# Router logits from a second, transposed copy of the input, and a first stage in a written order

## The chip, the cores and the metric

The kernel runs on one core of a Trainium2 chip, as one program. The metric is the device time in microseconds of that core: 2810.78 us, the median of three runs (2807.64 to 2812.17).

## The reference, cut to what matters

The input `x` has 32 batches of 128 x 1024 values in fp32. Two layers follow each other, each added to its own input.

```python
def _L0_cond_ref(x, conditions, weights):
    w = weights[conditions]                      # one 128 x 128 matrix per batch
    return jnp.einsum('bct,bcd->bdt', x, w)      # h = w^T x, per batch

def _moe(hidden_states, gate_w, wg, wu, wd):     # E = 64 experts, K = 8, CAP = 256
    logits = x @ gate_w.T                        # x here is h, 4096 tokens x 1024
    probs = jax.nn.softmax(logits, axis=-1)
    w, sel = jax.lax.top_k(probs, K)
    w = w / jnp.sum(w, axis=-1, keepdims=True)
    ...                                          # each expert takes its first 256 tokens
    h = silu(inp @ wg) * (inp @ wu)
    out = h @ wd                                 # scattered back, weighted by w

x = x + moe(cond(x))
x = x + L1_ffn(L1_cond(x))                       # dense 1024 x 1024 maps with low-rank terms
```

In the second layer two linear maps follow each other, `L1_cond_W` and the maps of `L1_ffn` (the kernel calls these side by side `head_w`). The kernel multiplies the two sets of weights with each other once, and applies the product to the tokens. These products of weights are called the combined weights here; they have nothing to do with the tokens.

## The kernel before, in words

A token is a row of `h`; a batch gives 128 tokens. The work has three stages.

**First stage** (lines 228 to 352). It runs over 8 groups of 4 batches. For a batch, GpSimd fetches the 128 x 128 matrix `w_b` by an indirect DMA, and the SP queue loads `x_t` (512 KB). The input is copied to `ybuf` in device memory, which collects the layer's sum. TensorE computes `h = w_b^T x` in two halves of 512 columns (`ph`, line 271), ScalarE copies both halves out (line 272), and the result is stored to `hbuf`, from which the experts gather their tokens. For the router logits the hidden size must lie on the partitions, so TensorE turns each of the 8 column blocks of `h` (`pt`, line 280), VectorE copies them out as `hT` (line 281), and 8 matmuls per batch with `hT` as the stationary operand give `plog` (line 283). Once per group come the top 8 of 64 logits, the weights `wt`, the ranks of the tokens within each expert (`prk`, lines 322 and 325), their store to `ranks`, and the counts (`pcnt`, line 333), which are added up in `upto`.

The combined weights are made in blocks of columns. Blocks 0 and 1 belong to this stage (lines 344 to 352): 9 products of 8 matmuls each per block (`pcw`, line 210). They are written last in the source, in order; a scheduler puts single matmuls of them between the batches' work. Their results gather in one tile, `CWa`, which a DMA stores to `cwbuf` once per block (line 352). A third block is made much later.

Order: of this stage nothing is kept in the order of the source. The scheduler may move an instruction on its engine wherever its operands allow. Instructions wrapped by `kept` or by the class `InOrder` (lines 213 to 225) stay in the order in which the source issues them; before, of these early parts only the VectorE object `dve` and the indirect DMAs of the lookup are wrapped, from the second stage on.

**Between the stages** (lines 575 to 603) the kernel finds which tokens the first experts take: `looked_up` (VectorE, from `upto`), `fetched` (8 indirect DMAs from `ranks`), `found` (VectorE, and one small matmul `prow`, line 438, that brings the row numbers to the right partitions), `placed`, `gathered` (8 indirect DMAs from `hbuf` per expert), and `columns` (VectorE turns the gathered tokens into `xT`). `token_sums` and `weight_sums` form the sums of half blocks with which the 8 products of a 2 x 2 block multiplication become 7 (`s`, `t` tiles).

**Second stage**: a loop over 64 experts, TensorE products `pp` (line 519) and `po` (line 630), with a prefetch of the next expert's three weights of 1.5 MB into tiles of two buffers per tag, `wg`, `wu` and `wd`. The operands of the combined weights use the same tags, so an expert's weight loads wait until these are read. **Third stage**: 16 pairs of batches through the second layer; neither changes.

Of the kernel before, what the change touches and what calls it, by code (L numbers as in the profile page):

```python
# [9 lines left out]
I32 = mybir.dt.int32  # L10
# [41 lines left out]
def kernel(  # L52
# [6 lines left out]
    gate_wT: bass.AP,  # L59
# [65 lines left out]
    for q in range(1, NQ):  # L125
# [22 lines left out]

    adapter_i = const.tile([P, NB], I32, name="adapter_i")
    nc.sync.dma_start(adapter_i, adapter.to_broadcast([P, NB]))  # L150
    scal_bc = const.tile([P, E2], F32, name="scal_bc")
    nc.sync.dma_start(scal_bc, scal.to_broadcast([P, E2]))
    adapter_rows = const.tile([P, NB], I32, name="adapter_rows")
    nc.vector.tensor_scalar(adapter_rows, adapter_i, float(P), pcol, ALU.mult, ALU.add)
    adapter_f = const.tile([P, NB], F32, name="adapter_f")
    nc.vector.tensor_copy(adapter_f, adapter_i)
    smask = const.tile([P, NB, E2], F32, name="smask")
    nc.vector.tensor_tensor(
        smask,
        adapter_f.unsqueeze(2).to_broadcast([P, NB, E2]),  # L160
        iota_t[:, 0:E2].unsqueeze(1).to_broadcast([P, NB, E2]),
        ALU.is_equal,
    )
    nc.vector.tensor_tensor(
        smask, smask, scal_bc.unsqueeze(1).to_broadcast([P, NB, E2]), ALU.mult
    )

    own = const.tile([P, HC], F32, name="own")
    nc.vector.tensor_scalar(own, iota_t[:, 0:HC], float(Q), inquad, ALU.mult, ALU.add)
    far = const.tile([P, 1], F32, name="far")  # L170
    nc.vector.tensor_scalar(far, quad, float(W4), None, ALU.mult)
    nc.vector.tensor_scalar(own, own, far, None, ALU.add)

    rb_bc = const.tile([P, E2], F32, name="rb_bc")
    nc.sync.dma_start(rb_bc, router_b.to_broadcast([P, E2]))
# [30 lines left out]
    def multiplied(n, d, hw, left, pool, tag, pe):  # L206
        w = BLOCKS[n][1] - BLOCKS[n][0]
        pcw = pool.tile([P, 512], F32, name=f"pcw_{n}_{d}", tag=tag)[:, 0:w]
        for j in range(HC):
            pe.matmul(pcw, left[d][:, j, :], hw[:, j, :], start=(j == 0), stop=(j == HC - 1))  # L210
        return pcw
# [13 lines left out]
    dve = InOrder(nc.vector)  # L225


    with (
        tc.tile_pool(name="a1", bufs=1) as a1,
        tc.tile_pool(name="a3", bufs=3) as a3,  # L230
        tc.tile_pool(name="a2", bufs=2) as a2,
        tc.tile_pool(name="pa_big", bufs=3, space=PSUM) as pa_big,
        tc.tile_pool(name="pa_sm", bufs=2, space=PSUM) as pa_sm,
        tc.tile_pool(name="pa_cw", bufs=2, space=PSUM) as pa_cw,
    ):
        gw_sb = a1.tile([P, HC, E], F32, name="gw_sb")
        nc.sync.dma_start(gw_sb, gate_wT.rearrange("(j p) e -> p j e", p=P))

        zeros = a1.tile([P, 256], F32, name="zeros")
        nc.vector.memset(zeros, 0.0)  # L240
        for buf in (hbuf, ybuf):
            nc.scalar.dma_start(
                buf[NT : NT + P, :].rearrange("p (n c) -> p n c", c=256),
                zeros.unsqueeze(1).to_broadcast([P, H // 256, 256]),
            )
        pad = a1.tile([E, 2, P], F32, name="pad")
        nc.vector.memset(pad[:, 0, :], float(NT))
        nc.vector.memset(pad[:, 1, :], 0.0)
        nc.scalar.dma_start(ranks[:, NB, :, :], pad)

        for g in range(NB // GB):
            plog = pa_sm.tile([P, GB, E], F32, name=f"plog_{g}", tag="sm")
            for t in range(GB):
                b = g * GB + t
                rows = slice(b * P, (b + 1) * P)
                w_b = a3.tile([P, P], F32, name=f"w_{b}", tag="w_b")
                nc.gpsimd.indirect_dma_start(
                    out=w_b,
                    out_offset=None,
                    in_=cond_w,  # L260
                    in_offset=bass.IndirectOffsetOnAxis(ap=cond_rows[:, b : b + 1], axis=0),
                )
                x_t = a3.tile([P, H], F32, name=f"x_{b}", tag="x_t")
                nc.sync.dma_start(x_t, x[b])
                nc.scalar.dma_start(ybuf[rows, :], x_t)

                h_sb = a2.tile([P, H], F32, name=f"h_{b}", tag="h_sb")
                for n in range(2):
                    cols = slice(n * 512, (n + 1) * 512)
                    ph = pa_big.tile([P, 512], F32, name=f"ph_{b}_{n}", tag="big")  # L270
                    nc.tensor.matmul(ph, w_b, x_t[:, cols], start=True, stop=True)  # L271
                    nc.scalar.copy(h_sb[:, cols], ph)
                nc.scalar.dma_start(hbuf[rows, :], h_sb)

                hT = a2.tile([P, HC, P], F32, name=f"hT_{b}", tag="hT")
                for n in range(2):
                    pt = pa_big.tile([P, 4, P], F32, name=f"pt_{b}_{n}", tag="big")
                    for j in range(4):
                        c = n * 4 + j
                        nc.tensor.transpose(pt[:, j, :], h_sb[:, c * P : (c + 1) * P], ident)  # L280
                    nc.vector.tensor_copy(hT[:, n * 4 : n * 4 + 4, :], pt)
                for j in range(HC):
                    nc.tensor.matmul(  # L283
                        plog[:, t, :],
                        hT[:, j, :],
                        gw_sb[:, j, :],
                        start=(j == 0),
                        stop=(j == HC - 1),
                    )
# [744 lines left out]
```

## Time and profile before

| What | Value |
|---|---|
| Median of 3 runs | 2810.78 us |
| The profiled execution: its own time, its span | 2809.41 us, 2807.7 us |
| Mean granted TensorE clock | 0.993 |
| Busy share of the span: TensorE, VectorE, ScalarE, GpSimd | 98%, 57%, 15%, 40% |
| HBM read, written | 442.90 MB, 123.83 MB |
| `ph` matmuls up to 310 us (records, busy) | 128, 69.0 us |
| `plog` matmuls up to 310 us | 512, 61.2 us |
| `pt` transposes up to 310 us | 256, 38.9 us |
| `pcw` matmuls up to 310 us | 288, 102.9 us |
| `hT` copies on VectorE, `h` copies on ScalarE | 64 x 688 ns, 64 x 587 ns |

The span runs from the first to the last instruction of the profiled execution; its own time is 1.7 us longer than the span. A line of a view names the source line, the engine, the tile written and the tile read. An fp32 matmul stands as two records, a transpose as one. A record's busy time [...] overlaps the next record, so how long a row of matmuls takes is read from the distance between their starts, or from the chain of waits, and not from busy times.

### The profile page before, as it was taken

To read this page: it belongs to the slowest core of one execution; us is meant where nothing else is said; L and a number is where in the kernel's file an instruction comes from. 1 tells how busy PE (TensorE), PEld (TensorE's weight loads), DVE (VectorE), ACT (ScalarE), POOL (GpSimd) and SP (SyncE) were. 2 spreads that over 40 slices of the span, in tenths; PEclk is the share of its full clock that TensorE was granted. 3 is DMA by queue.
4 is the path that set the end of the run, shared out by engine and by line. 5 is a ranking of instruction groups with operands and counts; after the bars stand their busy time and mean duration, and the time that the engine had idled before them with its cause. 6 is when DMAs were issued, how large, how long until landed. Compare 5 with 4: busy or idle time off the path is not lost.

```text
span 2807.7 us, 23998 instructions
## 1 busy us (share of the span) xinstructions
PE 2744.9 (98%) x8772; PEld 1516.8 (54%) x8772; DVE 1598.3 (57%) x2545; ACT 427.2 (15%) x824; POOL 1112.2 (40%) x846
## 2 busy tenths in 40 slices
PE   6998999999999999999999999999999899999999
PEld 4774555555555555555555555555555545555554
DVE  2443566676666766667666666666664344444443
ACT  1220111111111111112111111111111000000000
POOL 1114164655646555464554655556451100000000
PEclk9999999999999999999999999999999999999999
DMA  9873577877878787787877877778775532222210
GB/s 354 309 268 131 177 250 228 252 252 236 255 226 253 243 243 259 224 254 234 247 259 232 253 227 245 255 236 258 221 241 160 135 75 64 64 64 64 64 46 38
DMA packets 130789, 568.33 MB, mean 202 GB/s; under 512 B 23600, under 2 KB 50288, under 8 KB 105328
## 3 DMA queue, kind: packets, MB, share of 16 engines
q1 hardware_dynamic: 67040, 373.72, 36.7%
q0 software_dynamic: 51200, 155.24, 23.7%
q10 hardware_dynamic: 12432, 37.85, 3.5%
q8 instruction: 69, 1.13, 0.2%
q14 instruction: 48, 0.39, 0.0%
HBM read 442.90 MB, written 123.83 MB: 202 GB/s over the span
## 4 chain that ended last, share of the span: by engine, by line
PE 95%; DMA 3%; issue 1%; DVE 1%; POOL 0%; ACT 0%; SPq 0%; ACTq 0%; DVEq 0%
PE pp L519 41%; PE po L630 23%; PE pr_c L223 17%; PE pcw L210 3%; PE px L223 2%; PE pcw L223 2%; PE plog L283 2%; PE ph L271 2%; PE pth L569 1%; PE pt L280 1%; DMA hbuf<-h 1%; DMA hw<-in_head_w 1%; PE prk L325 0%; PE prk L322 0%; DMA xq<-ybuf 0%
## 5 line engine op out<-in xcount | busy, mean ns | idle before, releaser
L456 POOL DMA_INDIRECT xin<-hbuf,slot_row x512 | 715.1, 1397 | 209.1 <-issue 152.7
L630 PE MATMUL po<-wd,hTb 128*128 128x512 f32 x1536 | 680.3, 592 | 0.6 <-ACT hTb L571 0.6
L641 POOL DMA_INDIRECT ybuf<-o,slot_tok x128 | 204.3, 1596 | 665.2 <-ACT o L639 468.0
L630 PEld LDWEIGHTS po<-wd,hTb 128*128 128x128 f32 x1536 | 286.8, 190 | 323.7 <-issue 306.1
L519 PE MATMUL pp<-wg,xT 128*128 128x384 f32 x1024 | 351.3, 486 | 0.0
L519 PE MATMUL pp<-t,s 128*128 128x384 f32 x1024 | 344.6, 490 | 5.2 <-DVE t L223 5.2
L519 PEld LDWEIGHTS pp<-t,s 128*128 128x128 f32 x1024 | 194.6, 191 | 148.8 <-issue 31.2
L519 PEld LDWEIGHTS pp<-wg,xT 128*128 128x128 f32 x1024 | 189.6, 190 | 119.0
L223 DVE TENSOR_TENSOR u<-p,pp 128x384 f32<-128x384 f32 x64 | 35.4, 553 | 381.4 <-PE pp L519 381.4
L639 ACT ACTIVATE o<-po,slot_w 128x512 f32<-128x512 f32 x256 | 175.9, 687 | 494.5 <-PE po L630 494.5
L223 POOL DMA_INDIRECT ab<-in_AT,adapter_rows x32 | 36.5, 1142 | 449.4 <-ACT pxw L223 444.0
L223 PE MATMUL pr_c<-BM,X 128*128 128x512 f32 x480 | 213.7, 592 | 0.0
L223 DVE STREAM_TRANSPOSE xT<-xin 128x1024 f32<-128x1024 f32 x128 | 155.9, 1233 | 75.5 <-DMA xin<-hbuf,slot_row 65.0
L519 PE MATMUL pp<-t,xT 128*128 128x384 f32 x512 | 175.6, 486 | 0.0
L519 PE MATMUL pp<-wu,xT 128*128 128x384 f32 x512 | 175.6, 486 | 0.0
L519 PE MATMUL pp<-wu,s 128*128 128x384 f32 x512 | 175.6, 486 | 0.0
L536 ACT ACTIVATE h<-gate 128x384 f32<-128x384 f32 x128 | 67.0, 523 | 704.7 <-DVE gate L223 704.7
L392 POOL DMA_INDIRECT rkg<-ranks,row x128 | 123.1, 962 | 71.9 <-issue 38.4
L223 PE MATMUL pr_c<-ts,ss 128*128 128x512 f32 x320 | 142.5, 592 | 1.3 <-DVE ss L223 1.3
L223 PEld LDWEIGHTS pr_c<-BM,X 128*128 128x128 f32 x480 | 88.9, 190 | 100.2 <-issue 100.0
L223 DVE TENSOR_TENSOR u<-u,pp 128x384 f32<-128x384 f32 x128 | 70.4, 550 | 126.9 <-PE pp L519 126.9
L519 PEld LDWEIGHTS pp<-t,xT 128*128 128x128 f32 x512 | 97.3, 190 | 67.8
(159 smaller groups left out, 2990.4 us busy)
## 6 DMA issues: line engine op xcount, KB each, us to landing
wd<-in_wd SPq DMA_DIRECT2D x64, 1536.0 KB, 7.3
wg<-in_wg SPq DMA_DIRECT2D x64, 1536.0 KB, 6.9
wu<-in_wu SPq DMA_DIRECT2D x64, 1536.0 KB, 9.4
x<-in_x SPq DMA_DIRECT2D x32, 512.0 KB, 5.1
ybuf<-x ACTq DMA_DIRECT2D x32, 512.0 KB, 4.9
hbuf<-h ACTq DMA_DIRECT2D x32, 512.0 KB, 5.5
xq<-ybuf SPq DMA_DIRECT2D x64, 256.0 KB, 5.1
out_y<-out_c SPq DMA_DIRECT2D x32, 512.0 KB, 2.7
```

Of the source, the lines that this page charges most:

```text
L210: pe.matmul(pcw, left[d][:, j, :], hw[:, j, :], start=(j == 0), stop=(j == HC - 1))
L223: return lambda *args, **kw: kept(op(*args, **kw))
L271: nc.tensor.matmul(ph, w_b, x_t[:, cols], start=True, stop=True)
L280: nc.tensor.transpose(pt[:, j, :], h_sb[:, c * P : (c + 1) * P], ident)
L283: nc.tensor.matmul(plog[:, t, :], hT[:, j, :], gw_sb[:, j, :], start=(j == 0), stop=(j == HC - 1),)
L392: nc.gpsimd.indirect_dma_start(out=some["rk"][:, s, :, :].rearrange("p i t -> p (i t)"), out_offset=None, in_=ranks.rearrange("e b i t -> ...
L456: nc.gpsimd.indirect_dma_start(out=xin[:, q, :], out_offset=None, in_=quarters, in_offset=bass.IndirectOffsetOnAxis(ap=slot_row[:, s : s + ...
L519: nc.tensor.matmul(bank, left[k][:, j, :], right[k][:, j, :], start=(j == 0), stop=(j == HH - 1))
L536: nc.scalar.activation(h, gate, AF.Sigmoid)
L630: nc.tensor.matmul(po, hT[j][:, i, :], wd_sb[:, i, cols], start=(i == 0), stop=(i == IC - 1),)
L639: nc.scalar.mul(o_sb[:, cols], po, slot_w[:, s : s + 1])
L641: nc.gpsimd.indirect_dma_start(out=ybuf, out_offset=bass.IndirectOffsetOnAxis(ap=slot_tok[:, s : s + 1], axis=0), in_=o_sb, in_offset=None ...
```

## The change

1. The host passes a second copy of `x`, `x_t`, with the 1024 columns of each batch on the partitions. The gate weights are passed in the layout of their tile.
2. Logits are formed as `w^T (x gate^T)`: 8 matmuls per batch with the transposed input as stationary operand give `pxg` (128 x 64 per batch), VectorE copies it out once per group (`xg`), and one matmul per batch with `w_b` gives `plog`. The transposes `pt` and the copies `hT` are gone.
3. Of the two halves of `h` ScalarE copies one, VectorE the other.
4. TensorE, ScalarE, VectorE and the indirect DMAs of the first stage are all issued through `InOrder`. A group's order is `logits`, 4 x `mixed` (with the store of the previous batch's input, `carried`, behind each), some products of block 0 (`combined`, 0, 1, 1, 1, 1, 1, 2, 2 of them), `scored` of the next group, `counted`.
5. Buffers: six `x` tiles and six `w_b` (three before), four of the transposed input, three `h_sb` (two before), four PSUM tiles for `ph` and `pcw` together, three for the small ones.
6. Block 1's nine products stand behind the last group, in a row, and the lookup and the gathers of the first two experts are issued between them. Each product's result has a tile of its own (`cw`) and a store of its own (200 KB); `CWa` is gone.
7. The store of `ranks` goes from the SP to the ScalarE queue. The constants of the second layer (`adapter_rows`, `smask`, `own`, `rb_bc`) are made behind the first stage.
8. `weight_sums(0)` comes ahead of `columns(0)` and `token_sums(0)`. The tiles of gathered tokens lie in the pool `fs`.

```diff
     def multiplied(n, d, hw, left, pool, tag, pe):
...
         for j in range(HC):
+            if j == HC // 2:
+                yield
             pe.matmul(pcw, left[d][:, j, :], hw[:, j, :], start=(j == 0), stop=(j == HC - 1))
-        return pcw
+        yield pcw
...
+        def loaded_turned(b):
+            xTs[b] = a6.tile([P, HC, P], F32, name=f"xTb_{b}", tag="xTb", bufs=4)
+            nc.sync.dma_start(xTs[b].rearrange("p j c -> p (j c)"), x_t[b])
...
+        def scored(g):
+            pxg = pa_sm.tile([P, GB, E], F32, name=f"pxg_{g}", tag="sm")
             for t in range(GB):
...
+                xT_b = xTs.pop(g * GB + t)
                 for j in range(HC):
-                    nc.tensor.matmul(
-                        plog[:, t, :],
-                        hT[:, j, :],
+                    pe.matmul(
+                        pxg[:, t, :],
+                        xT_b[:, j, :],
                         gw_sb[:, j, :],
...
+            xg = a2.tile([P, GB, E], F32, name=f"xg_{g}", tag="xg")
+            dve.tensor_copy(xg, pxg)
+            for b in range((g + 1) * GB, min((g + 2) * GB, NB)):
+                loaded_turned(b)
+            return xg
+
+        def mixed(b):
...
+            h_sb = a2.tile([P, H], F32, name=f"h_{b}", tag="h_sb", bufs=3)
+            for n in range(2):
...
+                ph = pa_big.tile([P, 512], F32, name=f"ph_{b}_{n}", tag="big")
+                pe.matmul(ph, ws[b], xs[b][:, cols], start=True, stop=True)
+                if n == 0:
+                    act.copy(h_sb[:, cols], ph)
+                else:
+                    dve.tensor_copy(h_sb[:, cols], ph)
+            act.dma_start(hbuf[rows, :], h_sb)
+
+        def carried(b):
+            act.dma_start(ybuf[b * P : (b + 1) * P, :], xs.pop(b))
+
+        def logits(g, xg):
...
+            for t in range(GB):
+                pe.matmul(plog[:, t, :], ws[g * GB + t], xg[:, t, :], start=True, stop=True)
...
+        def combined(n, d):
...
+            halves = multiplied(n, d, hws[n], lefts, pa_big, "big", pe)
+            next(halves)
+            yield
+            pcw = next(halves)
+            if d < HC:
+                cw = fs.tile([P, BW], F32, name=f"cw_{n}_{d}", tag="cw", bufs=3)[:, 0 : hi - lo]
+                act.copy(cw, pcw)
+                act.dma_start(cwbuf[:, d, lo:hi], cw)
+            else:
+                act.copy(G_sb[:, lo:hi], pcw)
+            yield
...
+        xg = scored(0)
+        hws = {0: head_block(0)}
+        lefts = left_block("a", 0, "wd")
+        for g in range(NG):
+            ex, mask = logits(g, xg)
+            for t in range(GB):
+                b = g * GB + t
+                mixed(b)
+                if b:
+                    carried(b - 1)
+                if t == 1:
+                    wt = weights_of(g, ex, mask)
+                if b + 6 < NB:
+                    loaded_batch(b + 6)
...
+            for _ in range((0, 1, 1, 1, 1, 1, 2, 2)[g]):
+                for _ in combined(*rest.pop(0)):
+                    pass
+            if g + 1 < NG:
+                xg = scored(g + 1)
+                if g == 0:
+                    lefts += left_block("a", 1, "wd")
+                    lefts += left_block("a", 2, "wu")
+                if g == 4:
+                    hws[1] = head_block(1)
+            counted(g, mask, wt)
+        part = {0: looked_up([0, 1, 2, 3])}
+        fetched(part[0], 4 * NJ)
+        carried(NB - 1)
+        gathers = {}
+        for d in range(HC + 1):
+            step = combined(1, d)
+            next(step)
+            if d == 2:
+                found(part[0], 0, 1)
+                placed(part[0])
+                gathers[0] = gathered(0)
+            elif d == 3:
+                found(part[0], 1, 2)
+                placed(part[0])
+                gathers[1] = gathered(1)
+            elif d == 4:
+                found(part[0], 2, 4)
+                part[1] = looked_up([4, 5, 6, 7])
+                fetched(part[1], 4 * NJ)
+            next(step)
...
+        for _ in weight_sums(0, *mine[:2], right):
+            pass
+        xT = columns(0, gathers[0])
         for _ in token_sums(0, xT, left):
             pass
-        for _ in weight_sums(0, *mine[:2], right):
-            pass
+        halves = gathers[1]
         p1 = first_product(0, left, right)
...
-        "gate_wT": a(L0_ffn_gate_w).T,
+        "x_t": a(x).reshape(NB, P, HC, P).transpose(0, 3, 2, 1).reshape(NB, P, H),
+        "gate_w": a(L0_ffn_gate_w).reshape(E, HC, P).transpose(2, 1, 0).reshape(P, -1),
```

`combined` gives way twice, once in the middle of its 8 matmuls and once behind its store, so what the last loop issues at d = 2, 3 and 4 stands on TensorE between the two halves of that product.

## The prediction

> **What bounds the kernel now.** I read the table of windows first, cut where the stages change: start, the groups, the last group, the lookup beside the rest of the combined weights, the wait for the first expert.
>
> ```profile
> 0.00:58.50 58.50, 34.83 (x160) 22.66 (x160) 14.39 (x48) 10.22 (x20) 10.46 (x22) 0.91 0.96 377
> 58.50:199.90 141.40, 140.84 (x835) 101.41 (x834) 59.58 (x184) 42.04 (x88) 21.68 (x23) 1.00 0.86 298
> 199.90:220.00 20.10, 20.10 (x123) 14.94 (x122) 6.26 (x22) 4.21 (x10) 0.00 (x0) 1.00 0.15 56
> 220.00:301.90 81.90, 69.46 (x211) 40.25 (x210) 20.91 (x63) 6.27 (x13) 31.10 (x32) 0.94 0.39 132
> 301.90:314.40 12.50, 7.26 (x23) 3.98 (x22) 5.89 (x5) 2.24 (x3) 0.00 (x0) 0.93 0.88 328
> ```
>
> Behind the window's length stand TensorE, its weight loads, VectorE, ScalarE and GpSimd, then the granted clock, the DMA share and GB/s. Until 58.5 us the DMA is the bound (0.96 busy, TensorE 34.8 of 58.5). From there TensorE is, without a gap, at 298 GB/s. From 220 to 302 the DMA is nearly empty (132 GB/s) while TensorE works off the combined weights. The chain of waits from 216 us shows this end:
>
> ```profile
> 219.79 0.45 PE pcnt L333 x2
> ...
> 231.90 0.40 PE prow L438 x2
> ...
> 253.36 0.59 PE prow L438 x2
> 253.95 6.79 PE pcw L210 x14
> 260.87 40.51 PE pcw L210 x124
> 301.41 0.49 ACT CWa L351
> 301.92 6.26 DMA cwbuf<-CWa
> 308.43 0.55 issue
> 308.98 1.76 DVE t L223
> 310.83 1.76 DVE wu L223
> 312.59 1.68 DVE t L223
> 314.41 15.69 PE pp L519 x40
> ```
>
> The last counts end near 220; the first product that needs a weight sum starts at 314.41. I call the first moment t0. Two waits of TensorE in this stretch, from the list of waits:
>
> ```profile
> PE prow L438 <- DVE byq L223: 12.4, 2, 10.5
> ...
> PE pp L519 <- DVE t L223: 5.2, 1, 5.2
> ```
>
> The second exists since the tile for `s` lies where `CWa` is still being stored; VectorE stands 47.9 us for that DMA, with the weight sums queued behind. From 314 us on, the 64 experts and the third stage keep TensorE full and their code is the same, so I price the change up to this point alone.
>
> **The tail, t0 to 314.41 = 94.6 us.** A `pcw` record steps by 40.51/124 = 0.327 us. Of the 288, the windows of line 210 hold 72 before 220 us, so 216 are left: 70.6 us. With the waits 12.4 and 5.2, and the first `pp` product (8 records, 2.6 us, ahead of the 5.2 us wait), that is 90.8; the remaining 3.8 is the lower clock (0.94) and the small matmuls. After the change nine products are left, 144 x 0.327 = 47.1 us, four `prow` matmuls about 1.4, the first `pp` 2.6: **51.1 us**. That is 43.5 saved if t0 stays. What hides the other work of the tail:
> - Lookup: in the trace the row numbers are ready 4.5 us behind the counts, then come 8 fetches at 1.25 us (0.95 busy, 0.30 issue), and the first `prow` runs 12 us behind the counts. In the new order `prow` stands behind 2.5 products, 13 us. It fits by 1 us; if the store of `ranks`, now on ScalarE's queue behind the stores of `h`, lands 4 us late, TensorE loses 3, for it is in order.
> - Gathers: 8 for expert 0 from 16 to 26 us behind t0, landing at 29; two transposes (2.4) and the sums of tokens (2.7) end at 36, weight sums (7.0) fit before, once `wg` of expert 0 is loaded. Its buffer comes free with block 0, before t0. Cover until 48: nothing on the path; without cover it would be what lies over 48.
> - `CWa`'s wait goes; single `cw` stores cost 0.33 us of issue each on ScalarE, idle here.
> - Weights of expert 1 load only once the last `pcw` has read its operands, as before, but expert 0 no longer waits 5.2 us beside them. They land 6.9 to 9.4 us after issue (page); VectorE wants them some 9 us after the last `pcw`. Queued behind it are the evictions of expert 0. I take 1 us, ends 0 and 3.
> - The second layer's constants (1.7 us of VectorE, three small loads on SP) move into the tail's cover. In the third stage the first load of `pxw` now waits for the gathers of the last expert, issued some 60 us earlier: 0.
>
> **The groups: TensorE.** Steps per record from the chain: `plog` 3.52/32 = 0.11, `pt` 0.88/8 = 0.11, `ph` about 0.43. Per group the change removes 32 `pt` (3.5 us), replaces `plog` by `pxg` at the same shape and count (7.0, unchanged), adds four `w^T xg` (8 records, 0.9) and takes 16 `pcw` records in place of about 8 (50 in 6.1 groups): +2.5. Sum -0.1 on 23.2 us per group. The whole new loop: `ph` 128 x 0.43 = 55, `pxg` 56, `plog` 7, `prk` and `pcnt` about 21, block 0 47: 186 us, and some 15 until the first `w_b`, gate weights and four turned inputs are in. TensorE alone would put t0 at **201**. The copy `xg` (0.42 us on VectorE) has the 2 us of `counted` as cover; without it 8 x 0.5 = 4 us. VectorE loses 32 copies of 0.69 us net, ScalarE 32 of 0.59; both are far from bound.
>
> **The groups: DMA.** What must move by t0: `x` and `x_t` 33.55 MB, `h` 16.8, `ybuf` 16.25, `w_b` 2.1, operands of the combined weights 7.9, zeros 1.05, `ranks` 2.1, `cw` 1.6, gate 0.3, and one `wu` of 1.57 that SP issues early: **83.2 MB**, against 65.4 MB up to 220 us before. So the new loop asks for 9.1 MB in 23 us per group, and is bound by the DMA. The rate decides; the trace gives it from three rows:
> - 10 to 60 us, DMA share full throughout:
>
> ```profile
> DMA packets 6096, 20.49 MB, mean 410 GB/s; under 512 B 594, under 2 KB 2642, under 8 KB 5710
> ```
>
>   At 410 GB/s: 203 us and 4 of start, t0 = **207**.
> - The first window above, 377 GB/s with its start included, and with TensorE and the stores stalling as they do under a full DMA: 83.2/0.377, t0 = **220.6**.
> - The second window: 298 GB/s at 0.86 of the time; scaled to a full share 347: 240 and 4, t0 = **244**.
>
> I take 377: it is the only row in which loads, stores and waits of this very loop press on the DMA. The Trainium skill ("DMA: Bandwidth & Descriptors", Specifications) speaks against the change: about 358 GB/s of HBM for each core. By it t0 = 232 + 4 = 236 and 16 us of the gain would be lost. The row shows 410 over 50 us with one core at work, so the row decides; the rule stays in the range.
>
> A second rule speaks against it: "TensorE: Matmul & The Clock Gate" (Why this matters for your kernels) warns of idle gaps over some 3 us between bursts of matmuls, after which the clock falls to half. A loop that waits for the DMA has such gaps. At half clock for half the time the 186 us would be 279, and the kernel slower. In the first window, where TensorE idles 40% of the time, the granted clock is 0.91: 186/0.91 = 204 and 15, t0 = 219, still no more than the DMA's. I take the row.
>
> **Sum.** t0 = 220.6, tail 51.1, expert 1's weights 1: 272.7 instead of 314.4, so **41.7 us less**. The profiled execution took 2809.4 us: 2767.7. It lies 1.4 us under the median of the runs, within their spread; I say **2768**.
>
> **The rivals.**
> 1. *The DMA runs at its full rate.* For: prefetch of six `x` and four turned tiles keeps it fed. Against: 16 us per group in which no `h` is made, so stores come in bursts. t0 = 201 to 207: 55 to 61 us less, 2752.
> 2. *The mixed traffic runs at 347 to 358.* For: the groups' own row. Against: there TensorE was the bound. 18 to 26 us less, 2784 to 2792.
> 3. *Slower: in-order stores hold up TensorE.* All stores are issued by ScalarE, whose copies stand in fixed order behind them; a store that waits for an earlier transfer holds the next copy of `h`, its PSUM tile, and the matmuls behind. In the list of waits ScalarE's copy waits 19.6 us for stores of `h`, in 5 cases, up to 5.0 us. If it costs 1.5 us per batch on top of rival 2, t0 passes 262, at 318 GB/s, and the gain is gone; at 300 GB/s t0 = 277 and the time 2825. Against: three `h_sb`, and VectorE takes half the copies.
> 4. *The change does not do what it says for the time:* the tail becomes bound by lookup and gathers (late `ranks`, then gathers that end some 18 us behind block 1) and the loop ends at 244: both gains are used up, 2805 to 2815.
>
> **How the numbers follow.** My case 0.55 (own range 2755 to 2782), rival 1 0.15, rival 2 0.18, rival 3 0.09, rival 4 0.03. A measurement of this kernel tells 0.2% (5.6 us) from no change. Faster 0.88, within 0.03, slower 0.09. The range takes in rivals 1 and 2: 2747 to 2794.
>
> **What would show it.** The groups end at about 220 us with the DMA at 370 GB/s or more and TensorE at 0.8 to 0.9 busy; then `pcw` for 47 us without a wait for `byq`; `pp` on `t`, `s` within 1 us of the first `pp`; experts and third stage as long as before. Wrong: groups longer than 30 us each, ScalarE waiting for `hbuf<-h` in every batch, a granted clock near a half, or a `prow` wait of over 3 us.

## The result and the profile after

The changed kernel takes **2776.22 us** (median of four runs, 2774.86 to 2778.05) where the kernel before, beside it, takes 2809.57 us (four runs, 2807.64 to 2812.17). The ratio is 0.9881, with a 95% interval of 0.9864 to 0.9898: 33.4 us or 1.2% faster. 2768 was predicted, with a range of 2747 to 2794. The profiled execution took 2778.05 us, with a span of 2776.3. From here on `x_t` is the transposed copy of the input, and not the tile of that name in the kernel before.

The tail is as predicted, the loop is not. First the table of windows of the changed kernel, cut at the end of the start, where the last load of `x` is issued (206.5 us), at the last counts and at the first `pp` on `t`, `s` (columns as before: length, TensorE, weight loads, VectorE, ScalarE, GpSimd, granted clock, DMA share, GB/s):

```profile
0.00:31.00 31.00, 23.90 (x87) 19.06 (x88) 7.15 (x33) 3.85 (x8) 10.01 (x22) 1.00 0.77 287
31.00:206.00 175.00, 159.65 (x765) 113.89 (x763) 46.24 (x164) 29.65 (x68) 22.71 (x24) 0.90 1.00 386
206.00:234.80 28.80, 28.80 (x145) 19.77 (x145) 7.49 (x27) 6.17 (x14) 0.00 (x0) 1.00 0.65 243
234.80:285.80 51.00, 50.51 (x160) 29.57 (x159) 32.51 (x78) 4.60 (x10) 34.45 (x33) 1.00 0.65 220
```

The loop ends at t0 = 234.8, 14.2 us later than the 220.6 of the prediction. It has three stretches with different bounds. Up to 31 us neither TensorE nor the DMA is full. From there to 206 us the DMA is (share 1.00, 386 GB/s), while TensorE idles 15 us and has a granted clock of 0.90. From the issue of the last load of `x` on, TensorE is full for 28.8 us and the DMA is not. The summary of the DMA up to 232 us has the bytes of the prediction (83.2 MB), at a mean rate below its 377 GB/s:

```profile
DMA packets 25543, 83.18 MB, mean 359 GB/s; under 512 B 3519, under 2 KB 7673, under 8 KB 25017
```

Cut at each group's `plog`, the same table shows where the time went. These are groups 1 to 4, each with one product of the combined weights:

```profile
43.00:78.30 35.30, 29.81 (x122) 20.46 (x123) 6.70 (x23) 5.85 (x13) 3.77 (x4) 0.81 1.03 416
78.30:113.00 34.70, 27.74 (x123) 20.96 (x123) 7.49 (x27) 4.55 (x11) 3.89 (x4) 0.80 1.00 394
113.00:135.70 22.70, 22.70 (x125) 16.30 (x124) 7.49 (x27) 4.91 (x12) 3.89 (x4) 1.00 0.92 332
135.70:163.60 27.90, 26.30 (x124) 19.03 (x122) 7.48 (x27) 4.92 (x12) 3.90 (x4) 0.88 1.00 387
```

A group in which TensorE never waits takes 22.7 us (23.1 in the prediction's step). Groups 1 and 2 take 35.3 and 34.7, and there the clock is 0.8. Of the 12.0 us that group 2 takes beyond 22.7, 7.0 are its wait for `x_t`, and 5.1 what its narrow matmuls take longer behind it. The chain of waits says how a group comes to be late, and what a wait costs on top of itself:

```profile
6.58 13.90 PE pxg L206 x64
...
36.20 19.49 DMA ybuf<-zeros
55.71 5.34 DMA ybuf<-x
61.06 0.33 SPq L339
...
61.49 9.24 DMA xTb<-in_x_t
...
70.78 3.15 PE pxg L206 x16
73.92 3.61 PE prk L206 x16
...
126.23 7.09 PE pxg L206 x64
133.32 1.89 PE prk L206 x16
```

The store of the zero rows lands at 55.69 us, and a store of `x` is issued at 55.71; only when this has landed may the next `x` be loaded into that buffer (L339), and an `x_t` load stands behind it on SP's queue. That the one store waits for the other has a reason that holds for all of this stage: the loads of SP and the stores of ScalarE share eight semaphores. Up to t0 a semaphore is taken again 149 times in this trace, each time only after the transfer that had it before has landed, and 51 times within 0.15 us of that. So no more than eight of these transfers are under way at once, and a load can wait for a store with which it shares nothing else.

Compare the rows of `pxg`: the same 64 records take 7.09 us at 126 us, and 13.90 at the start. `prk` takes 1.89, or 3.61 behind a wait. The tail then goes without a hole. This is TensorE's timeline; in brackets stands what it idled for:

```profile
234.91 13.20 PE L206 MATMUL pcw<-hw,WB_a 128*128 128x388 f32 x40
248.60 0.39 PE L206 MATMUL prow<-byq,spread 128*128 128x8 f32 x2 [0.49 <-DVE byq L206]
...
259.72 23.71 PE L206 MATMUL pcw<-hw,WB_a 128*128 128x388 f32 x72
283.26 2.74 PE L591 MATMUL pp<-wg,xT 128*128 128x384 f32 x8
285.84 5.32 PE L591 MATMUL pp<-t,s 128*128 128x384 f32 x16
```

Both waits of TensorE that the prediction named are gone (0.49 us is left of 12.4), and `pp` on `t`, `s` follows the first `pp` at once: 51.0 us from t0, where the tail took 94.6. In sum the loop is some 15 us longer and the tail some 43 shorter (28.6 at this point); the way to expert 1 is 0.9 shorter (30.85 in place of 31.8), the experts take 29.1 us each as before, and the third stage is 1.9 shorter. That is the 31.4 us between the two spans.

### The profile page after: what moved, and what is told of

Same layout as the page of the kernel before. It is cut to its first block, busy times and chain, and to the rows that moved or that the text cites. A ratio compares the mean times of both kernels' runs of the same rounds, so it can differ in the third digit from the quotient of the medians.

```text
span 2776.3 us, 23659 instructions
## 1 busy us (share of the span) xinstructions
PE 2733.0 (98%) x8580; PEld 1515.0 (55%) x8580; DVE 1580.4 (57%) x2521; ACT 408.1 (15%) x792; POOL 1110.6 (40%) x846
## 4 chain that ended last, share of the span: by engine, by line
PE 94%; DMA 3%; DVE 1%; issue 1%; ACT 0%; ACTq 0%; SPq 0%; POOL 0%; DVEq 0%; POOLq 0%
PE pp L591 41%; PE po L690 23%; PE pr_c L206 17%; PE pcw L206 4%; PE px L206 2%; PE pxg L206 2%; PE pth L641 2%; PE ph L206 1%; DMA xTb<-in_x_t 1%; DMA ybuf<-zeros 1%; PE prk L206 1%; DMA ybuf<-x 1%; DMA wu<-in_wu 0%; PE pg L206 0%; PE pt L206 0%
## 5 line engine op out<-in xcount | busy, mean ns | idle before, releaser
L591 PEld LDWEIGHTS pp<-wu,xT 128*128 128x128 f32 x512 | 97.3, 190 | 67.8
```

What stands on the lines that cost most here:

```text
L591: nc.tensor.matmul(bank, left[k][:, j, :], right[k][:, j, :], start=(j == 0), stop=(j == HH - 1))
```

## The experiments

Times are medians. The kernel before took 2809.64 in the first series (e1, e3, e4, e5), 2811.38 in the second (e2, e8, e9, e10), 2808.22 and 2807.76 in the last two. The changed kernel was not run again beside them. Since the kernel before moves by 3.6 us from series to series, a difference of a few us to the changed kernel counts only where the trace shows where it arises.

### The two halves of the change

**Order alone.** The written order, buffers and tail, but logits from a transposed `h`, without `x_t`:

```diff
-                xg = scored(g + 1)
+                if t:
+                    turned_h(b - 1)
+                if t > 1:
+                    scored_h(b - 2)
...
+                    pe.transpose(pt[:, j, :], hs[b][:, c * P : (c + 1) * P], ident)
+                dve.tensor_copy(hT[:, n * 4 : n * 4 + 4, :], pt)
```

> The written order, the buffers and the tail of the changed kernel, but the logits as before: h is turned by TensorE in 8 blocks per batch, VectorE copies them out, 8 matmuls per batch follow. No transposed input is loaded; 66.4 MB instead of 83.2 move up to the last counts. If the transposed layout is what gains (it takes 3.5 us of transposes per group off TensorE and 44 us of copies off VectorE): slower than the changed kernel, by 2 us per group, 2790 or more. If the gain lies in the order and the tail, and the layout costs more in DMA than it saves on TensorE: TensorE-bound groups of about 24.7 us from the start, last counts at 212 to 222 us, the kernel at 2758 to 2768 us, faster than the changed one.

Measured: 2790.20 us, ratio 0.9932 (0.9916 to 0.9949). t0 is 246, the tail again 51 us. The counts of its even groups stand 26.57 us apart:

```profile
90.14 0.70 PE L206 MATMUL pcnt<-mask,ones 128*128 128x256 f32 x2
116.71 0.70 PE L206 MATMUL pcnt<-mask,ones 128*128 128x256 f32 x2
143.28 0.70 PE L206 MATMUL pcnt<-mask,ones 128*128 128x256 f32 x2
```

The order, with its buffers, brings the tail. Its loop is 3.9 us per group longer than the undisturbed group of the changed kernel: the 32 transposes (3.5 us by the prediction's rows) and a wait of up to 0.8 for `hT`.

**Logits alone.** The old free order, tail and buffers (but six `w_b` in place of three), with logits as w^T (x gate^T):

```diff
-                        nc.tensor.transpose(pt[:, j, :], h_sb[:, c * P : (c + 1) * P], ident)
-                    nc.vector.tensor_copy(hT[:, n * 4 : n * 4 + 4, :], pt)
...
+                xT_b = a3.tile([P, HC, P], F32, name=f"xTb_{b}", tag="xTb", bufs=4)
+                nc.sync.dma_start(xT_b.rearrange("p j c -> p (j c)"), x_tr[b])
...
+                nc.tensor.matmul(plog[:, t, :], wbs[t], xg[:, t, :], start=True, stop=True)
```

> The kernel before, with its free order, its buffers and its tail, but logits as w^T (x gate^T) from the transposed input. If the layout is a gain of its own: TensorE's groups lose the 3.5 us of transposes and add 0.9, the scheduler fills the place with products of block 0, last counts no later than before (220 us) and the kernel 10 to 20 us faster than before. If the extra 16.8 MB cost more than the transposes save: last counts 10 to 25 us later than before, some of it given back because more products are done by then, and the kernel between 5 us faster and 15 us slower than before.

Measured: 2816.57 us, ratio 1.0021 (1.0014 to 1.0029): 6.9 us slower than before. Its waits of TensorE:

```profile
PE ph L274 <- DMA x<-in_x: 18.2, 10, 2.8
PE pxg L281 <- DMA xTb<-in_x_tr: 11.6, 1, 11.6
PE prow L439 <- DVE byq L224: 8.0, 2, 6.1
PE pp L520 <- DVE t L224: 5.1, 1, 5.1
```

With three `x` tiles of prefetch TensorE waits 18.2 us for `x`, and both waits of the old tail are still there. Each half alone gives -19.4 and +6.9; together they give -33.4. So the layout gains time only together with the written order and its buffers; which of these two it needs was not separated.

### Is it the bytes?

**x_t loaded once.** `x_t` is loaded for the first four batches only and used again for all groups, so the logits of the other groups are those of the first group's `x`; the stores and the other loads are as in the changed kernel:

```diff
+            if b >= GB:
+                xTs[b] = xTs[b - GB]
+                return
```

> The changed kernel, but the transposed input is loaded for the first four batches alone, and all groups take their logits from these four tiles: 14.7 MB less are read, the matmuls and stores are the same in number and order. Left out is the right choice of experts, so the output differs. Theory A and B (the DMA bounds part or all of the groups): last counts at 202 to 212 us instead of 234.8, the kernel 23 to 32 us faster than the changed one, 2744 to 2753. Theory C (stores in ScalarE's order): the stores are the same, so at most 8 us faster. Theory D (TensorE's lower clock behind its waits): the waits for the transposed input go and with them the half clock, so as A.

Measured: 2757.99 us, ratio 0.9818 (0.9801 to 0.9834), 18.2 less than the changed kernel. t0 is 215.2 and the tail 51.0. So the loads of `x_t` cost 19.6 us of the loop. In the window from 31 to 206 us the DMA now has a share of 0.86 and TensorE is busy 166.6 of 175: with 14.7 MB less TensorE is the bound again. Of the 14 us over the 201 that the prediction had for TensorE alone, 7.1 are one wait for ScalarE's copies of `prk` (at 67 us); half rate behind it and at the start takes part of the rest.

**Operands loaded late.** The operands that the loop needs late (two parts of the combined weights' left side, the second block's columns, the zero rows, expert 0's weights) are loaded late, and every load of SP keeps its written order:

```diff
-                if g == 0:
+                if g == 2:
                     lefts += left_block("a", 1, "wd")
+                if g == 4:
                     lefts += left_block("a", 2, "wu")
-                if g == 4:
+                if g == 6:
                     hws[1] = head_block(1)
...
-            if g == 0:
+            if g == 5:
                 for buf in (hbuf, ybuf):
...
-            nc.sync.dma_start(xs[b], x[b])
+            kept(nc.sync.dma_start(xs[b], x[b]))
```

> The changed kernel, with the second and third part of the operands of the combined weights loaded behind group 2 and group 4, block 1's columns behind group 6, the zero rows stored behind group 5, the first expert's weights behind these, and the loads of SP kept in the order of the source. No bytes and no computation change. Theory A (two bounds take turns: groups 1 and 2 take 35 us each at 416 and 394 GB/s since about 8 MB that are needed late are loaded there, and the later groups are bound by TensorE at 22.7 us): groups 1 and 2 fall to 25 to 29 us, the later ones stay under 25, the last counts come at 220 to 226 us instead of 234.8, the kernel takes 2762 to 2768 us. Theory B (the total of 83 MB at a sustained 359 GB/s sets the end, whenever what is loaded): the last counts stay within 3 us of 234.8 and the time at 2774 to 2779. Theory C (stores that wait in ScalarE's fixed order hold TensorE up): as B, since the stores are the same.

Measured: 2830.17 us, ratio 1.0076 (1.0059 to 1.0093), slower than before the change. Theory A was wrong here by over 60 us, because the edit changed two things. The chain of waits shows the second, which comes in five of the groups; here are two:

```profile
88.41 3.63 DMA ybuf<-x
92.52 8.75 DMA xTb<-in_x_t
101.40 13.89 PE pxg L206 x64
115.29 3.61 PE prk L206 x16
...
125.00 3.71 DMA ybuf<-x
129.20 8.79 DMA xTb<-in_x_t
138.12 13.89 PE pxg L206 x64
```

In the written order the last `x` load of a group, which waits for the store of the tile that it replaces, stands ahead of the next group's four `x_t` loads. TensorE then waits 5.1 us in such a group, and the wait costs more than itself: `pxg` takes 13.89 us in place of 7.09 and `prk` up to 3.61 in place of 1.89. Such a group takes 36 us, with the DMA at 0.74. Behind the 5.1 us of waiting another 8.5 us are lost to half rate.

**x_t first.** The same with the `x` load written one batch later, behind the store that it waits for, so that `x_t` loads never stand behind a waiting `x` load; once with the operands as early as in the changed kernel, once with them late:

```diff
                     carried(b - 1)
+                    if b + 5 < NB:
+                        loaded_x(b + 5)
```

> Edit on the changed kernel: the loads of x, of x_t and of the combined weights' operands keep their written order on SP's queue, and the load of an x tile is written one batch later (tile b+5 in batch b, just behind the store of the tile whose buffer it takes), so that the four x_t loads of the next group always stand ahead of the x loads that wait for a store. The same bytes move, and the operands are still asked for as early as in the changed kernel. Theory Q (the loop lost its time because x_t loads stood on SP's in-order queue behind x loads that wait for the store of the tile they replace): TensorE's waits for x_t (7.0 us at most) go, groups 1 and 2 shrink from 35 us each to 23 to 27, the last counts end at 208 to 216 instead of 234.8, time 2750 to 2758. Theory A (the operands that are loaded early make groups 1 and 2 DMA-bound): groups 1 and 2 stay at 32 to 35 us, time 2770 to 2778. Theory B (83 MB at a sustained 359 GB/s set the end): no change, 2774 to 2778.

> As the run before it, and the operands that are needed late (parts 1 and 2 of the combined weights' left side, the second block's columns, the zero rows, the first expert's weights) are loaded where they are needed: behind groups 2, 4, 6, 5 and the loop. It undoes the confusion of the first late-operands run, in which the x_t loads stood behind waiting x loads in every group. Theory Q: within 4 us of the run before it, 2748 to 2756. Theory A: this is the edit that brings the gain, 2750 to 2758, 12 or more below the run before it. Theory B: 2774 to 2778, since the bytes are the same. Were the order of SP's queue of no weight, this would come out near the first late-operands run, 2830.

Measured: 2773.02 us, ratio 0.9865 (0.9847 to 0.9883), and 2771.79, ratio 0.9861 (0.9843 to 0.9879). Theory Q falls: in the first, TensorE's waits for `x_t` are all but gone, but what it waited for has only changed its name:

```profile
PE ph L206 <- DMA x<-in_x: 8.2, 4, 4.7
...
PE pxg L206 <- DMA xTb<-in_x_t: 0.6, 1, 0.6
```

t0 is 232.2, 2.6 us earlier. A full DMA (389 GB/s from 31 to 206 us) delays whatever is asked for last. With the operands late as well, t0 is 225.0, but only 4.4 us of 9.8 arrive at the end: the first row of `ranks` is fetched 10.2 us behind the counts and not 6.5, and `prow` waits 4.57 us for VectorE where it waited 0.49. The tail takes 56.7 us. This is the step of the prediction that "fits by 1 us", seen to fail.

**Another tile stored.** What goes to `ybuf` is read from the gate weights' tile and not from `x`, so the output lacks `x`; the bytes are the same, and the buffer of an `x` tile is free as soon as its products have run:

```diff
-            act.dma_start(ybuf[b * P : (b + 1) * P, :], xs.pop(b))
+            xs.pop(b)
+            act.dma_start(
+                ybuf[b * P : (b + 1) * P, :].rearrange("p (n c) -> p n c", c=HC * E),
+                gw_sb.rearrange("p j e -> p (j e)").unsqueeze(1).to_broadcast([P, 2, HC * E]),
+            )
```

> Edit on the changed kernel: what is stored into ybuf for each batch is taken from the gate weights' tile (twice 512 columns) and no longer from the x tile, so the output lacks x; the same bytes move, but an x tile's buffer is free as soon as its two products have run, and no x load waits for a store. Theory Q (the chain from the store of an x tile to the next x load, and the x_t loads behind it on SP, sets the loop): the last counts end 12 us or more sooner, 2750 to 2765. Theory S (a full DMA sets it): the loads can only run ahead of the stores by the six buffers, 3 MB or 7 us: 2768 to 2777.

Measured: 2794.69 us, ratio 0.9956 (0.9939 to 0.9973). t0 is 232.5, 2.3 us earlier, and the DMA is as full as before (398 GB/s from 31 to 206 us), as theory S has it. The edit takes away one chain from stores to loads, and not all: through the shared semaphores, loads of `x` and `x_t` stand 50.5 us on SP's queue for stores of `h`, in 15 waits. The time is another 18 us longer than the changed kernel's, for a reason that lies in the tail and that no theory had (below).

### Is it the clock at the start?

**Warm start.** Four 128 x 512 matmuls on constants ahead of the first group, in the 6.6 us in which TensorE has no operands:

```diff
+        for _ in range(4):
+            pe.matmul(
+                pwarm, ident, ident.unsqueeze(1).to_broadcast([P, 4, P]), start=True, stop=True
+            )
         xg = scored(0)
```

> Edit on the changed kernel: four 128x512 matmuls on constants, whose result nobody reads, stand ahead of the first group's x_t products, in the 6.6 us in which TensorE waits for its first operands. Theory D (the first 64 narrow products run at half rate, 13.9 us instead of 7.1, since the clock is low behind the wait, and that is lost for good): they take 7.1 to 10 us, and the time falls by 4 to 7 us, 2769 to 2772. Theories A and B (the DMA sets the end of the loop): the first group starts earlier and waits longer later, 2774 to 2778. Theory Q: between the two, since the chain from the stores of the first x tiles starts earlier.

Measured: 2769.71 us (2768.76 to 2771.93), ratio 0.9855 (0.9837 to 0.9872). TensorE's timeline:

```profile
1.53 6.70 PE L206 MATMUL pwarm<-ident 128*128 128x512 f32 x8 [1.53 <-POOL ident masks.py:199]
8.07 7.25 PE L206 MATMUL pxg<-gw_sb,xTb 128*128 128x64 f32 x64
```

The 64 records of `pxg` take 7.25 us where they took 13.89, and t0 is 226.3, 8.5 us earlier, with the same tail of 51.2. Theories A and B had said no change. The DMA shows why it is not hidden. Here are its first 31 us, in the columns of the table of windows:

```profile
0.00:31.00 31.00, 28.95 (x161) 21.06 (x162) 8.10 (x34) 4.44 (x9) 11.48 (x23) 1.00 0.94 354
```

In the changed kernel it was 287 GB/s, and between 24 and 31 us 128, where here it is 407. One wait of SP's queue makes that gap in the changed kernel:

```profile
SPq L179 <- DMA hbuf<-h: 9.5, 1, 9.5
```

This is the load of `hw`. Its buffer is free, but it has the semaphore of the first store of `h`, and is issued at 30.32 us, as that store lands (30.30); TensorE at half rate lets the store begin only at 27.3. In the warmed kernel the semaphores fall otherwise, `hw` is issued at 16.8 us, and the next 1.6 MB of operands at 20.6 in place of 30.8. So the edit takes away two things at once, TensorE's half rate and a wait of 3.2 MB of loads; what each of them is worth was not separated. Together they give back more than half of the 14.2 us.

### Is it the work that is left at the end?

**Products early.** The nine products between the groups are spread in another way:

```diff
-            for _ in range((0, 1, 1, 1, 1, 1, 2, 2)[g]):
+            for _ in range((0, 2, 2, 2, 1, 1, 1, 0)[g]):
```

> Edit on the changed kernel: the nine products of the first block of combined weights that stand between the groups are spread as 0, 2, 2, 2, 1, 1, 1, 0 over groups 0 to 7 in place of 0, 1, 1, 1, 1, 1, 2, 2. Same bytes, same instructions. Theory S (two bounds in series: the DMA is full from 31 us until the last inputs land near 206 us, and only then TensorE works off what is left, among it two products of 5.2 us each in the last group): products moved to groups 1 to 3 run there in TensorE's waits for x_t, the last group shrinks by 10.4 us, and the last counts end 5 to 11 us sooner: 2765 to 2771. Theory B (the bytes at one sustained rate set the end): 2774 to 2778. A third way, the early groups are not bound by the DMA and take the 10.4 us that the late ones give: no change, 2774 to 2778.

Measured: t0 = 221.6, 13.2 us earlier, more than the expected 5 to 11: three products (15.6 us) now run in groups 1 to 3, while TensorE would have waited for the DMA. For the loop that is theory S. But the time is 2786.00 us, ratio 0.9924 (0.9908 to 0.9941), 9.8 more than the changed kernel, since the tail takes 74.5 us in place of 51. In TensorE's timeline:

```profile
258.29 0.58 PE L206 MATMUL pcw<-hw,WB_a 128*128 128x388 f32 x1 [0.92 <-issue]
259.70 0.49 PE L206 MATMUL pcw<-hw,WB_a 128*128 128x388 f32 x1 [0.84 <-issue]
260.43 0.58 PE L206 MATMUL pcw<-hw,WB_a 128*128 128x388 f32 x1 [0.24 <-issue]
261.83 0.49 PE L206 MATMUL pcw<-hw,WB_a 128*128 128x388 f32 x1 [0.82 <-issue]
```

From 257 to 287 us a record starts each 0.7 or 1.4 us and not each 0.33, and the idle time is put down to "issue": TensorE waits for nothing that the profile shows.

**With a warm start**, all nine products early, or one only moved from each of the last two groups (0, 1, 2, 2, 1, 1, 1, 1); and a warm start with the late operands:

> The run before it and the four 128x512 matmuls on constants ahead of the first group (alone they took 6.5 us off: 2769.7). If the one shortens the end behind the last inputs and the other the empty stretch of the DMA at the start (theory S), they add up: 2758 to 2765. If both only fill the same waits, 2765 to 2770.

> Edit on the changed kernel: the four 128x512 matmuls on constants ahead of the first group, and only one product each moved from groups 6 and 7 to groups 2 and 3 (0, 1, 2, 2, 1, 1, 1, 1). Theory S (DMA first, then TensorE, in series): the last counts end 13 to 17 us sooner than in the changed kernel, 217 to 222. What is asked is the tail: in the two runs with the products moved early it took 73 to 75 us in place of 51, since TensorE then issued its products' instructions one or two per 0.7 us for 15 to 29 us, with no wait shown. If that comes with last counts that end early (theory F), it comes here too and the time is 2778 to 2786; if it hangs on how many products stand in the last group (0 in both), or on chance in the timing of the transfers, it does not come, and the time is 2759 to 2765, the best of all kernels.

> The late operands with x_t loads first, and the four matmuls on constants ahead of the first group. If the queue's order is the cause and TensorE then sets the loop (theory Q), the start's half clock is on the path, and this is 4 to 7 us below the run without the four matmuls: 2742 to 2751. If the DMA sets the loop even then (theories A and B), no difference from it (under 2 us).

Measured: 2781.64 us, ratio 0.9907 (0.9890 to 0.9923), with t0 = 216.7 and a tail of 73.3; 2785.96, ratio 0.9923 (0.9907 to 0.9940), with t0 = 222.1 and a tail of 70.2; and 2768.77 (2766.83 to 2771.82), ratio 0.9850 (0.9832 to 0.9867), with t0 = 223.5 and a tail of 57.1. In the loop the two gains nearly add up (18.1 us with both, 8.5 and 13.2 alone), and they are lost in the tail. The second of the three comes out where theory F put it, but the tail does not go by early counts (below). Beside late operands the warm start is worth 3.0 us, less than the 4 to 7 of theory Q and hardly more than the spread, for the runs of the two kernels overlap; t0 is 1.5 us earlier. This last kernel and the warm start alone end 7.5 and 6.5 us below the changed kernel; their runs and its runs do not overlap, though the intervals of the ratios do.

## Why the prediction was right and where it was wrong

- **The tail: right.** 51.1 us was the sum of 144 records, four `prow` and the first `pp`; 51.0 was measured, and 50.8 to 51.2 in four more kernels with the same tail (e2, e3, e4, e8). A small error cancels in it: there are three `prow`, of 0.5 us in all, and a wait of 0.5, where four of 1.4 us were summed. The margin of 1 us for `prow` is real: e9 and e10 overran it.
- **`CWa`'s wait and expert 1's weights: right, nearly.** The 5.2 us went with it, and stay in the kernel that changes the logits alone (5.1). `wu` of expert 1 lands 11.5 us after its issue (6.9 to 9.4 was taken), and TensorE idles 1.1 us for it, as the sum said; a clock of 1.00 in place of 0.92 more than pays for that.
- **TensorE per group: right.** 22.7 us where 23.1 was worked out, in the groups without a wait.
- **The bytes: right,** and the DMA's rate too: 386 GB/s in the stretch where it is full, against the 377 that was taken. The 358 GB/s that the Trainium skill gives for each core ("DMA: Bandwidth & Descriptors", Specifications) would have put t0 at 236, near the 234.8 measured, but not for its reason: the rate while the DMA is full is higher, and the mean of 359 comes from the stretches where it is not.
- **The failed step: "is bound by the DMA. The rate decides".** All 83.2 MB were divided by one rate, and t0 was the larger of two totals. The end is left out of that, and the start is in it only as the old kernel had it (351 GB/s in its first 31 us). The rate itself was not too high: at the 386 GB/s of the full stretch the bytes would take 216 us. To these the two ends add 19. At the start 8.9 MB are moved in 31 us, 8 us more than at the full rate; in this time SP stands 9.5 us at the load of `hw`. At the end 28.8 us of TensorE's work stand behind the issue of the last load of `x`, with 7 MB to be moved in them, 11 us more than at the full rate. Between the ends the other 67.6 MB take 175 us. Both ends were tested: e2 shortens the first (-8.5 us), e11 the last (-13.2), with all bytes still moved. So of the terms it is t0 that was mis-sized, 220.6 for 234.8, and the mechanism named for it (a loop bound by the DMA) holds in its middle.
- **The clock: the wrong side was chosen.** The prediction weighed the granted clock of 0.91 against a rule of the skill ("TensorE: Matmul & The Clock Gate", Why this matters for your kernels) by which waits of some 3 us between bursts put the clock at half, and took the row. The row reads too high: the trace of the kernel before has no entry of the clock ahead of 19.2 us, and the column counts a stretch without an entry as 1.00, while four records of `ph` take 3.78 us at 10.84 us and 1.88 at 40.87. The rule's direction holds here: behind waits of 5.1 us `pxg` runs at half rate (e1), and at the start of every kernel but the warmed ones. Waits shorter than the rule's were enough too, where they fell among narrow matmuls: 0.72 us in group 1 and 1.45 in group 4. It is not the doubling of the whole loop that the prediction set against the row. Half rate costs 10 us at the start (6.8 in `pxg`, the rest in `plog` and `ph`), 3.4 each behind the waits of groups 1 and 4, and 5.1 in group 2 (the rows of `pxg`, `prk` and `pcnt` against those of group 3); two shorter stretches of group 1 are not counted. TensorE's sum hides the start's loss by luck: 15 us were taken until its operands are in, where 6.6 were measured, so that with the first `pxg` it came to 22.0 us, and 21.0 were measured.
- **The rivals.** The DMA at its full rate came near in rate (386 GB/s where 410 was taken) and not in time. The mixed traffic at 347 to 358 would give 2784 to 2792, and the mean rate, 359, was just above that; its reason fails as above. Stores that hold up TensorE: it waits 3.4 us for stores of `h` in all. A tail bound by the lookup did not come here, but came in part in e9 and e10.

**What stays open.** In e11, e12, e13 and e14 TensorE issues some of its tail's products in steps of 0.7 us or multiples of it, for 11 to 30 us, and the tail takes 70 to 75 us, part of it waits of `prow` of 2 to 6 us. All runs of these kernels are as long as their profiled ones, so it is in all of them. e13 has the changed kernel's instructions of TensorE in the same order, so it is not a wait that the order adds. In e13 VectorE too stands 7.6 us for "issue" in the tail (until 257.6 us), and TensorE's slow stretch (from 270 us on) ends as the DMA table shows a transfer of an instruction queue (282 to 284 us); in e11 such a transfer stands at 254 to 256 us, ahead of the slow stretch. In e12 and e14 it stands at 251 and 255 us, ahead of the slow stretches at 259 and 260. Late instructions are a guess that fits the first and not the others. It does not go with an early t0 (232.5 in e13; 215.2 in e3, without it). No run was made that takes it away.

## What to carry to other kernels

Two bounds do not overlap at the ends of a loop: add what the DMA loses before it is full, and what it loses behind the last load, where the engine works off the rest, to the time of the bytes at the full rate, instead of taking the larger of two totals. A wait of TensorE ahead of narrow matmuls costs more than its length: 5.05 us of it cost 13.6 in e1, and 0.7 us among them some 4 in group 1. A few wide matmuls in a gap at the start are cheap. Where an empty stretch of the DMA has no full buffer behind it, look at whose landing its queue waits for: a shared semaphore can tie a load to a store. And when waits move from one transfer to another while the time hardly moves (as from `x_t` to `x` in e8), the DMA as a whole is the bound, and the order of its queue is not.

## What the runs showed that was not expected

**Narrow matmuls did not bring the clock back; wider ones did.** In e1 64 records of 128 x 64 behind a 5.05 us wait run back to back for 13.89 us at 0.217 us each, the `prk` behind them (128 x 128) are still slow, and the granted clock is 0.50 for 18.5 us from the start of the burst:

```profile
101.40:119.90 18.50, 18.50 (x83) 17.88 (x84) 0.42 (x1) 1.64 (x3) 0.00 (x0) 0.50 0.58 219
```

By the entries of the clock in the traces, full rate comes back 2.1 to 4.6 us after the first `prk` in the five groups of e1 that waited, however many narrow records ran before (64 at half rate), and 3.3 to 4.5 us after it in groups 1, 2 and 4 of the changed kernel (10 to 32). At the start of the changed kernel it comes at 27.0 us, 4.3 us after the first `ph` (128 x 512) and 20.4 after the first `pxg`. In e2 6.7 us of 128 x 512 matmuls are enough: the next record runs at 0.11 us.

**The column of the clock has a blind start.** It shows 1.00 for the first 31 us all the same, since the trace has no entry of the clock before 27.0 us. There the length of a record tells more than the column.

**One core alone** moves 386 to 389 GB/s of loads and stores together for 175 us on end, and 416 over the 35 us of one group.

**The step of 0.7 us** in TensorE's issue, above, is the last of these.
